# A graph-and-attention layer: seven of the eight q blocks made by seven products of halves, put together by VectorE

## The chip, the cores and the metric

The kernel runs on one core of a Trainium2 chip. The metric is the device time of one execution in microseconds (us); the kernel before has a median of 1512.12 us over three runs (1512.09 to 1512.35). Everything is float32. Engines are named as in the profile: PE is TensorE, DVE is VectorE, ACT is ScalarE, POOL is GpSimd, SP is the queue that issues most DMAs.

## What is computed

The input is x (4096 rows of 256) and a dense adjacency matrix of 4096 by 4096. Cut to what matters:

```python
h = layernorm(x) @ neigh_W.T
h = adj @ h / (adj.sum(axis=1, keepdims=True) + 1)
x = x + concat([layernorm(x), h]) @ lin_W.T        # the graph part

y = layernorm(x)                                   # one sequence of 4096
h = rmsnorm(y)
q, k, v = h @ wq.T, h @ wk.T, h @ wv.T             # 4 q heads, 2 k/v heads, 64 wide
q = q * cos + rotate_half(q) * sin                 # k likewise
att = causal softmax(q k / 8) v
y = y + att @ wo.T
out = x + y + mixture_of_8_experts(rmsnorm(y))     # the two best of a softmax router
```

rotate_half swaps the two halves of 32 of a head and negates the first.

## The kernel before

The 4096 rows are cut into eight blocks of 512. The first stage makes the graph part and, in its shadow, q, k and v; then follow attention and the experts. The change lies in the first stage alone, which on the timeline ends at about 510 us.

The stage is a loop over eight row blocks b. For each, `aggregate(b, steps)` (L516) adds up the products of eight adjacency blocks of 512x512, one for each step jb. A step does not make eight products of quarter blocks but seven (the scheme of Strassen and Winograd): `halve(n)` (L484) lets VectorE make the four sums S1, S2, S4 and S3 of a block's quarters (L495 to L498, each 128x512), S3 in place of A21; the g tiles hold the features and their sums. Each of the seven products is taken in two parts, k = 0 and 1 (L538), and in the profile each part is two instructions. The products fall into four PSUM banks. Steps 0 and 7 take the order `BY_BANK`, products 1, 2, 6, 7, 5, 3, 4, so that a bank after the other is done; they read A11, A12, S2, S3, S1, S4 and A22. At the end VectorE puts the seven together (L546 to L560).

The schedule is written out by hand: `tc.manual_schedule()` keeps every engine's instructions in the order of the code. In `aggregate` a step first calls `halve` for the block after it, so that VectorE makes the sums one step ahead; it then issues the seven products, and after the fourth it calls the functions that `steps` lists for this step. At the step's end come those listed under "end", the load of the adjacency block three further (three buffers, on SP), and those under "loaded".

What is listed for aggregate b is `qkv(b - 1)` (L573), which turns the row block just finished into q, k and v: step 1 the scales and tables, step 2 `norm` and `leave` (the normed rows go out to DRAM in `turning`), after step 2 `fetch` (they come back as 32x32 squares into `z`, which is room of a later qT, or `last_z` for b - 1 = 6), after step 3 `turn` (VectorE transposes z into qT[b], which now holds the normed rows with their features on the partitions), step 4 `values_and_logits` and `turned_heads((2,))` for k, step 5 `turned_heads((0, 1))` for the two halves of q. The eighth row block is made after the stage, in another way, by `rotated` and `heads`; the change does not touch it.

`turned_heads` (L644) makes 128 features of q or k by two products of 128x512 (L648) into a PSUM bank pj. VectorE multiplies pj by the cosines into its place, `to` (L655). ScalarE copies pj in four pieces of 32 partitions, swapped and with signs, into the tile `rot` (L657), of which there is one buffer (`bufs=1`). GpSimd multiplies rot by the sines (L661) and adds it to `to` (L662). Here `to` is qT[b] itself for q; its old content, the normed rows, has been read by then.

PSUM beside the four banks of the sums: two buffers tagged pj (`p_pj`) and two tagged tr (`p_tr`). They go round: `linear` (L195) takes one of each per half block at the end of step 0, `values_and_logits` two tr in step 4, k one pj in step 4, q two pj in step 5.

Weights: `load_rest` and `scale_rest` bring wq, wk and wv into wqkv_sb during aggregate 0; its last listed function is `router_wo` in step 7.

## Time and profile before

| | |
|---|---|
| median of three runs | 1512.12 us |
| the profiled execution | 1511.47 us |
| its span, first to last instruction | 1509.8 us |
| granted TensorE clock | 0.999 |
| TensorE busy | 1496.9 us, 99% |
| VectorE busy | 1083.9 us, 72% |
| ScalarE busy | 544.9 us, 36% |
| GpSimd busy | 568.9 us, 38% |
| q's products (L648, with k's) | 84 instructions, 592 ns each from issue to end |
| one product of the sums (L538) | 1792 instructions, 379 ns each from issue to end |

The profile is of one execution. Matmuls overlap in the pipeline: the distance from one start to the next is shorter than the 379 or 592 ns of one. A timeline row merges like instructions that follow each other: start, length of the whole row, engine, line, operation, tiles out<-in, shape and count; in brackets stands the idle time of the engine ahead of it and what ended it. The busy shares are means over stages of different kinds.

### The profile page before, as it was taken

How to read it: one execution, taken by the hardware profiler on the slowest of the kernel's cores; microseconds unless marked ns; L12 is line 12 of the kernel's file. 1: busy time of each engine (PE TensorE's matmuls, PEld its weight loads, DVE VectorE, ACT ScalarE, POOL GpSimd, SP SyncE). 2: the span in 40 equal slices, each digit the busy share in tenths (PEclk: the TensorE clock that was granted, in tenths of full speed). 3: DMA queues.
4: the chain of work that ended last, by engine and by line, in shares of the span. 5: the costliest groups of instructions: out<-in, count | busy, mean ns of one | idle time of the engine just before them, and what ended most of it. 6: DMA issues, size and time to landing. Idle time of an engine off the chain costs nothing. (4 is left out here: it accounts for less than half of the span.)

```text
span 1509.8 us, 28585 instructions
## 1 busy us (share of the span) xinstructions
PE 1496.9 (99%) x10731; PEld 1102.8 (73%) x10731; DVE 1083.9 (72%) x2239; ACT 544.9 (36%) x975; POOL 568.9 (38%) x649
## 2 busy tenths in 40 slices
PE   9999999999999999999999999999999999999997
PEld 7888888888888544444444444358899999999996
DVE  7855666656765577779879879795676877777872
ACT  2102011021020455655665655653222334343341
POOL 2102122121221331374565553551523464554542
PEclk9999999999999999999999999999999999999999
DMA  7435645555566000011010110029977898999965
GB/s 244 133 119 178 201 147 173 166 170 171 162 184 185 21 15 22 24 59 30 30 59 28 36 41 30 30 87 336 251 180 225 254 278 233 264 272 246 270 155 135
DMA packets 127005, 220.56 MB, mean 146 GB/s; under 512 B 79530, under 2 KB 103338, under 8 KB 113226
## 3 DMA queue, kind: packets, MB, share of 16 engines
q1 hardware_dynamic: 113322, 200.39, 42.3%
q0 software_dynamic: 12720, 17.47, 6.6%
q8 instruction: 86, 1.41, 0.4%
q10 hardware_dynamic: 816, 0.79, 0.2%
q14 instruction: 61, 0.50, 0.1%
HBM read 188.67 MB, written 31.33 MB: 146 GB/s over the span
## 5 line engine op out<-in xcount | busy, mean ns | idle before, releaser
L826 PE MATMUL sc<-qT_all,kT 64*64 64x512 f32 (+3 forms) x2304 | 282.1, 557 | 0.5 <-ACT pt_all L834 0.3
L538 PE MATMUL acc<-a,g 128*128 128x256 f32 x1024 | 244.0, 379 | 0.0
L538 PEld LDWEIGHTS acc<-a,g 128*128 128x128 f32 x1024 | 194.1, 190 | 32.2 <-issue 6.7
L826 PEld LDWEIGHTS sc<-qT_all,kT 64*64 64x64 f32 x2304 | 91.3, 133 | 128.9 <-issue 109.9
L834 ACT ACTIVATE pt_all<-sc 128x1024 f32<-128x1024 f32 (+3 forms) x157 | 149.0, 956 | 99.9 <-PE sc L826 95.6
L1917 POOL DMA_INDIRECT acc_dram<-y,late x40 | 63.3, 1583 | 177.0 <-ACT y L1906 118.9
L538 PE MATMUL acc<-more_sums,g 128*128 128x256 f32 x512 | 126.3, 379 | 0.0
L854 DVE TENSOR_TENSOR late<-late,pt_all 128x1024 f32<-128x1024 f32 (+3 forms) x92 | 106.6, 1159 | 20.4 <-ACT pt_all L834 9.0
L661 POOL TENSOR_TENSOR rot<-rot,tables 128x512 f32<-128x512 f32 x21 | 34.4, 1636 | 192.4 <-ACT rot L657 137.3
L538 PEld LDWEIGHTS acc<-more_sums,g 128*128 128x128 f32 x512 | 97.2, 190 | 13.2
L868 PE MATMUL y_second<-pt_all,vv 64*64 64x512 f32 (+3 forms) x440 | 105.0, 555 | 0.0
L868 PE MATMUL y_first<-pt_all,vv 64*64 64x512 f32 (+3 forms) x440 | 104.3, 553 | 0.0
L1837 PE MATMUL h<-late,qT_all 128*128 128x256 f32 (+1 forms) x616 | 104.0, 327 | 0.0
L1837 PEld LDWEIGHTS h<-late,qT_all 128*128 128x128 f32 x616 | 93.5, 191 | 9.6 <-ACT late L1521 0.8
L1110 POOL DMA_INDIRECT lists<-row,slots x64 | 91.3, 1426 | 17.2 <-issue 14.5
L636 ACT COPY vv<-pv 128x256 f32<-128x256 f32 x14 | 5.2, 373 | 251.9 <-PE pv L632 216.0
L868 PE MATMUL y_third<-pt_all,vv 64*64 64x512 f32 (+3 forms) x376 | 89.8, 557 | 0.0
L1844 DVE TENSOR_TENSOR late<-si,h 128x256 f32<-128x256 f32 (+2 forms) x87 | 39.3, 466 | 64.4 <-ACT si L1843 44.6
L657 ACT ACTIVATE rot<-pq 32x512 f32<-32x512 f32 x84 | 49.5, 589 | 82.5 <-DVE qT_all L655 33.1
L1843 ACT ACTIVATE si<-h 128x256 f32<-128x256 f32 (+2 forms) x87 | 36.1, 418 | 107.0 <-PE h L1837 93.1
L538 PE MATMUL acc<-qT_all,g 128*128 128x256 f32 x256 | 65.7, 379 | 0.0
L854 DVE TENSOR_TENSOR sum_all<-sum_all,pt_all 128x1024 f32<-128x1024 f32 (+3 forms) x49 | 53.5, 1093 | 15.8 <-POOL pt_all L836 9.9
(480 smaller groups left out, 3321.4 us busy)
## 6 DMA issues: line engine op xcount, KB each, us to landing
a<-in_adj_dram SPq DMA_DIRECT2D x64, 1024.0 KB
qT_all<-in_w_dram SPq DMA_DIRECT2D x18, 1408.0 KB
pt_all<-in_w_dram SPq DMA_DIRECT2D x16, 1408.0 KB
res_all<-in_w_dram SPq DMA_DIRECT2D x17, 768.0 KB
pt_all<-in_w_dram SPq DMA_DIRECT2D x16, 768.0 KB
res_all<-in_w_dram SPq DMA_DIRECT2D x8, 1408.0 KB
qT_all<-in_w_dram SPq DMA_DIRECT2D x9, 768.0 KB
late<-lists SPq DMA_DIRECT2D x96, 64.0 KB
```

The lines of the kernel that those rows point to most:

```text
L538: nc.tensor.matmul(acc[bank][:, at, :], g[jb][:, right, k, :], m[left][:, k, :], start=(jb == 0 and k == 0 and at == 0), stop=(jb == NB - ...
L657: nc.scalar.activation(rot[n * Q : (n + 1) * Q, :], pj[(n ^ 1) * Q : ((n ^ 1) + 1) * Q, :], AF.Copy, scale=1.0 if n % 2 else -1.0,)
L661: nc.gpsimd.tensor_mul(rot, rot, tables[b][:, 1, :])
L826: nc.tensor.matmul(ps[k * HP : (k + 1) * HP, j, :w], kT[sb][hd, i * P + k * HP : i * P + (k + 1) * HP], qT[b][hd, p, off:], start=True, st ...
L834: nc.scalar.activation(pt[:, :, :w], ps[:, :, :w], AF.Exp, scale=HD ** -0.5)
L854: nc.vector.tensor_add(sums[b, p][:, :, off:], before[:, :, off:], pt[:, :, : 512 - off])
L868: nc.tensor.matmul(accs[b, p][k][hd, off:], vv[sb][some, i, hd], pt[some, j, : 512 - off], start=(s == order_of(b)[0]), stop=(s == order_o ...
L1110: put = nc.gpsimd.indirect_dma_start(out=lists[:, :], out_offset=bass.IndirectOffsetOnAxis(ap=chosen[b][:, k, t, :], axis=0), in_=flats[b] ...
L1837: nc.tensor.matmul(ps[m % 2][:, m // 2 - q, :], w13_sb[:, c, m * P : (m + 1) * P], xT[:, c, :], start=(c == 0), stop=(c == 1),)
L1843: nc.scalar.activation(si[:, 0:both, :], ps[0][:, 0:both, :], AF.Silu)
L1844: nc.vector.tensor_mul(hT[:, q : q + both, :], si[:, 0:both, :], ps[1][:, 0:both, :])
L1917: put = nc.gpsimd.indirect_dma_start(out=(acc_dram if k < NM - LAST else out)[:, :], out_offset=at, in_=y[:, h, :], in_offset=None, comput ...
```

## The change

For row blocks 0 to 6 q is made by seven products of halves. The weights of q form a 2x2 of 128x128 pieces A11 to A22 (output half by input half), the normed rows a 2x2 of 128x256 pieces B11 to B22 (input half by columns). Once, in step 7 of aggregate 0, `sum_heads` has GpSimd make four sums of the weights. In step 4 of each following aggregate, ahead of the values, `sums_h` has VectorE make four sums of the rows in the room of z. In step 5 `seven_heads` takes the place of `turned_heads((0, 1))`: seven products of 128x256 into two pj and two tr banks; a copy by ScalarE and seven additions by VectorE, which write q over the rows in qT[b]; then the rotation of each half, which now reads q from SBUF: first ScalarE's four copies into rot, then VectorE's multiplication in place, then GpSimd's multiplication and addition. `last_z` becomes part of g[0], and the room freed holds the sums of the weights. k is made as before.

```diff
--- before.py
+++ after.py
@@ -386,6 +386,20 @@
             nc.scalar.copy(
                 wo_sb[:, :, C:], ps[:, 0 : 2 * NE].rearrange("p (j e) -> p j e", j=2)
             )
+
+        sums_q = gw.tile([P, 4, P], F32, name="sums_q")
+        heads_q = {
+            f"A{r + 1}{c + 1}": wqkv_sb[:, c, r * P : (r + 1) * P]
+            for r in range(2) for c in range(2)
+        }
+        heads_q.update((f"S{n + 1}", sums_q[:, n]) for n in range(4))
+
+        def sum_heads():
+            m = heads_q
+            nc.gpsimd.tensor_add(m["S1"], m["A21"], m["A22"])
+            nc.gpsimd.tensor_sub(m["S2"], m["S1"], m["A11"])
+            nc.gpsimd.tensor_sub(m["S3"], m["A11"], m["A21"])
+            nc.gpsimd.tensor_sub(m["S4"], m["A12"], m["S2"])
 
         def negate_weights():
             for k in range(2):
@@ -568,7 +582,7 @@
             )
 
         turning = [tc.dram_tile([512, C], F32, name=f"turning{n}") for n in range(2)]
-        last_z = gs.tile([P, 1024], F32, name="last_z")
+        last_z = g[0].rearrange("p n k i -> p (n k i)")[:, 0:1024]
 
         def qkv(b):
 
@@ -616,7 +630,7 @@
             def turn():
 
                 made["hT"] = qT[b]
-                z = made.pop("z").rearrange("p (m c d) -> p c m d", c=2, d=Q)
+                z = made["z"].rearrange("p (m c d) -> p c m d", c=2, d=Q)
                 for c in range(2):
                     nc.vector.transpose(
                         qT[b][:, c, :].rearrange("p (m i) -> p m i", i=Q), z[:, c]
@@ -640,6 +654,61 @@
                             first_lg[b][:, t, :], pj[:, i, 0:NE], AF.Copy,
                             scale=made["ratio"][:, t],
                         )
+
+            def sums_h():
+
+                m = made["m"] = {
+                    f"B{c + 1}{h + 1}": qT[b][:, c, h * 2 * P : (h + 1) * 2 * P]
+                    for c in range(2) for h in range(2)
+                }
+                room = made.pop("z").rearrange("p (n i) -> p n i", n=4)
+                m.update((f"T{n + 1}", room[:, n]) for n in range(4))
+                nc.vector.tensor_sub(m["T1"], m["B12"], m["B11"])
+                nc.vector.tensor_sub(m["T2"], m["B22"], m["T1"])
+                nc.vector.tensor_sub(m["T3"], m["B22"], m["B12"])
+                nc.vector.tensor_sub(m["T4"], m["T2"], m["B21"])
+
+            def seven_heads():
+
+                m = {**heads_q, **made.pop("m")}
+                banks = [
+                    p_pj.tile([P, 2, 2 * P], F32, tag="pj", name=f"pq_{b}_{n}") for n in range(2)
+                ] + [
+                    p_tr.tile([P, 2, 2, P], F32, tag="tr", name=f"pq_{b}_{n}").rearrange(
+                        "p c t i -> p c (t i)"
+                    ) for n in range(2, 4)
+                ]
+                p = {}
+                for n, (number, left, right) in enumerate((
+                    (1, "A11", "B11"), (2, "A12", "B21"), (6, "S2", "T2"), (7, "S3", "T3"),
+                    (5, "S1", "T1"), (3, "S4", "B22"), (4, "A22", "T4"),
+                )):
+                    p[number] = banks[n // 2][:, n % 2, :]
+                    nc.tensor.matmul(
+                        p[number], m[left], m[right], start=(n % 2 == 0), stop=True,
+                        skip_group_check=True,
+                    )
+                u2 = u4 = m["B12"]
+                u3 = m["B22"]
+                nc.scalar.copy(u2, p[1])
+                nc.vector.tensor_add(m["B11"], u2, p[2])
+                nc.vector.tensor_add(u2, u2, p[6])
+                nc.vector.tensor_add(u3, u2, p[7])
+                nc.vector.tensor_add(u4, u2, p[5])
+                nc.vector.tensor_add(m["B12"], u4, p[3])
+                nc.vector.tensor_sub(m["B21"], u3, p[4])
+                nc.vector.tensor_add(m["B22"], u3, p[5])
+                for k in range(2):
+                    to = qT[b][:, k, :]
+                    rot = gx.tile([P, 512], F32, tag="rot", name=f"rot_{b}_{k}", bufs=1)
+                    for n in range(4):
+                        nc.scalar.activation(
+                            rot[n * Q : (n + 1) * Q, :], to[(n ^ 1) * Q : ((n ^ 1) + 1) * Q, :],
+                            AF.Copy, scale=1.0 if n % 2 else -1.0,
+                        )
+                    nc.vector.tensor_mul(to, to, tables[b][:, 0, :])
+                    nc.gpsimd.tensor_mul(rot, rot, tables[b][:, 1, :])
+                    nc.gpsimd.tensor_add(to, to, rot)
 
             def turned_heads(ms):
                 pjs = [p_pj.tile([P, 512], F32, tag="pj", name=f"pq_{b}_{m}") for m in ms]
@@ -663,7 +732,7 @@
 
             return [
                 [scales, lambda: turn_tables(b)], [norm, leave], [],
-                [values_and_logits, lambda: turned_heads((2,))], [lambda: turned_heads((0, 1))],
+                [sums_h, values_and_logits, lambda: turned_heads((2,))], [seven_heads],
             ], {
                 (2, "end"): [fetch], (2, "loaded"): [lambda: spread_tables(b)],
                 (3, "end"): [turn],
@@ -705,7 +774,7 @@
                 steps[jb, "end"] = [lambda b=jb + 3: turned_x(b)]
         steps[0].insert(1, lambda: turned_x(2))
         steps[3].append(load_rest)
-        for jb, f in ((5, scale_rest), (6, bounds), (6, turn_wo), (7, router_wo)):
+        for jb, f in ((5, scale_rest), (6, bounds), (6, turn_wo), (7, router_wo), (7, sum_heads)):
             steps[jb].append(f)
         behind, at_end = [], []
         for b in range(NB):
```

## The prediction, made before the changed kernel was run

> **What bounds the kernel now.** I read the busy table and the groups first, to see who is never idle, then the timelines of four engines around one place where q is made. I chose the fifth of the seven (361 to 393 us): its adjacency block lands neither early nor late.

> ```profile
> PE 1496.9 (99%) x10731; PEld 1102.8 (73%) x10731; DVE 1083.9 (72%) x2239; ACT 544.9 (36%) x975; POOL 568.9 (38%) x649
> ...
> L661 POOL TENSOR_TENSOR rot<-rot,tables 128x512 f32<-128x512 f32 x21 | 34.4, 1636 | 192.4 <-ACT rot L657 137.3
> ...
> L657 ACT ACTIVATE rot<-pq 32x512 f32<-32x512 f32 x84 | 49.5, 589 | 82.5 <-DVE qT_all L655 33.1
> ```

> TensorE is the bound: 99% busy, so whatever its stream loses or gains is the kernel's time. In this stretch no TensorE row shows idle time at all, and q starts exactly 58.82 us after the one before (313.11, 371.93, 430.75). TensorE's timeline (start, us, row):

> ```profile
> 371.93 3.60 PE L648 MATMUL pq<-qT_all,wqkv_sb 128*128 128x512 f32 x8
> 375.36 1.03 PE L538 MATMUL acc<-a,g 128*128 128x256 f32 x4
> ...
> 383.13 2.75 PE L538 MATMUL acc<-a,g 128*128 128x256 f32 x12
> 385.72 1.03 PE L538 MATMUL acc<-more_sums,g 128*128 128x256 f32 x4
> 386.58 1.03 PE L538 MATMUL acc<-a,g 128*128 128x256 f32 x4
> 387.45 1.89 PE L538 MATMUL acc<-more_sums,g 128*128 128x256 f32 x8
> ```

> Each product of the program is two instructions. The row at 385.72 matters: it is the first in the last adjacency block (step 7) that reads a sum of VectorE's, S2; S3 is read at 386.58. VectorE's timeline:

> ```profile
> 374.70 0.69 DVE L655 TENSOR_TENSOR qT_all<-pq,tables 128x512 f32<-128x512 f32 x1 [3.59 <-PE pq L648]
> 375.56 0.69 DVE L655 TENSOR_TENSOR qT_all<-pq,tables 128x512 f32<-128x512 f32 x1 [0.17 <-PE pq L648]
> 376.17 0.68 DVE L495 TENSOR_TENSOR more_sums<-a 128x512 f32<-128x512 f32 x1
> 377.29 0.69 DVE L496 TENSOR_TENSOR more_sums<-more_sums,a 128x512 f32<-128x512 f32 x1 [0.44 <-PE acc L538]
> 378.02 0.69 DVE L497 TENSOR_TENSOR more_sums<-a,more_sums 128x512 f32<-128x512 f32 x1
> 378.62 1.76 DVE L498 TENSOR_TENSOR a<-a 128x512 f32<-128x512 f32 x1
> ```

> The sums for step 7 (L495 to L498) stand in VectorE's order directly behind the two rotation multiplies. S2 is ready at 377.98, 7.7 us ahead of its use. That 7.7 us is the cover to watch. ScalarE's and GpSimd's timelines:

> ```profile
> 375.51 2.39 ACT L657 ACTIVATE rot<-pq 32x512 f32<-32x512 f32 x4 [5.04 <-DVE qT_all L655]
> 381.54 2.39 ACT L657 ACTIVATE rot<-pq 32x512 f32<-32x512 f32 x4 [3.64 <-POOL qT_all L662]
> ```
> ```profile
> 378.05 1.79 POOL L661 TENSOR_TENSOR rot<-rot,tables 128x512 f32<-128x512 f32 x1 [4.47 <-DVE more_sums L496]
> 379.91 1.60 POOL L662 TENSOR_TENSOR qT_all<-qT_all,rot 128x512 f32<-128x512 f32 x1
> 384.07 1.54 POOL L661 TENSOR_TENSOR rot<-rot,tables 128x512 f32<-128x512 f32 x1 [2.56 <-ACT rot L657]
> ```

> rot has one buffer: ScalarE's second copy waits 3.64 us for GpSimd to finish with the first. Today only ScalarE and GpSimd carry that wait; VectorE's multiplies read PSUM and don't touch rot.

> [...]L498 takes 1.76 us beside L661 and 0.69 alone. [...]the rows above stand in the order of the code. [...]a ScalarE copy of 128x512 from PSUM took 586 ns (L439), one of 128x514 from SBUF 625 (L722).

> **The change, part by part.**

> TensorE's products. Out go 8 instructions of 128x512, 0.430 us apart ((3.60-0.592)/7), 3.44 us; in come 14 of 128x256, 0.216 apart ((2.75-0.379)/11), 3.02 us. Gain 0.42 us a block, 2.94 in seven. Weight loads rise from 8 to 14, 190 ns each, under the 216 between products as in L538's own rows.

> sum_heads: four GpSimd instructions of 128x128 once, in step 7 of aggregate 0. Between 0 and a 128x512's 1.27 us each; GpSimd sits idle for 20 us ahead of L661, so nothing waits[...]. Zero. last_z moved onto g[0]: fetch's DMAs are issued after step 2 and g[0] is last read in step 0; no queue waits. No DMA is added, and the tables' next load on SP comes at 390.74, after their last reader even in the case below.

> sums_h: four 128x256 adds ahead of kT's multiply (L655), some 1.7 us at 0.42 (rows L467 to L470). kT's multiply, ScalarE's rot and the release of its PSUM bank move back as much. That bank is the one that the third product of seven needs, 0.86 us after the start. Here: multiply to 369.7, ScalarE 369.8 to 372.2, needed at 372.79: no wait. In the first place (multiply 133.63 now, product 137.49) the wait is 1.1 us, in the third (250.84, 255.14) 0.6; the others have room. Together 1.7 us.

> The seven adds, and VectorE's new wait. The copy of p1 (0.37) and the first two adds hide behind the products. u3 overwrites B22, which the sixth product reads until 374.7. From there the critical chain:
> - u3, u4, B12: three adds 0.45 apart (as L547 to L549), to 376.1. ScalarE starts its first rot copy about there.
> - Four copies of 32x512, now from SBUF: 0.589 plus the 0.04 of the L722 comparison, 2.5 us, to 378.65. The in-place multiply of `to` must wait for them.
> - VectorE's multiply, GpSimd's multiply and add, then rot is free: 3.6 us (now 3.64), to 382.25.
> - Four copies of the second half, 2.5 us, to 384.75. VectorE's second multiply has been waiting at the head of its queue all this time; it ends at 385.5.
> - Only now S1 and S2 for step 7, queued behind it. GpSimd's multiply and add run just then, and the two engines take turns, as at 384.52 and 386.09 (1.64 and 1.75 us). S2 done 388.9, seen by TensorE at 389.0.

> TensorE, 0.42 ahead, wants S2 at 385.30: it stops for 3.7 us. S4 and S3 follow at 389.6 and 390.2, where S3 is wanted at 389.86: 0.45 more with the hand-over. So 4.15 us per block. Next late is L547, behind the next block's four sums (2.75 us), at about 393.4, and TensorE reaches its bank at about 393.6: just hidden. The last place has no following sums; the same otherwise.

> Sum: 7 × 4.15 + 1.7 - 2.94 = 27.8 us. The profiled execution took 1511.47 (span 1509.8 and 1.67 around it): 1539.3; it lies 0.65 under the median of 1512.12, so the forecast on that scale is 1540.

> **Bounds of what isn't shown.** Turn-taking: if GpSimd doesn't get between, S2 comes at 386.9 and the block loses 2.05 instead of 4.15: sum 13, or 1525. [...] ScalarE's SBUF copy: at its present 0.589, 0.3 us less a block; at double the extra, 0.3 more. Where ScalarE waits for all seven adds, not three, 0.8 more a block; where VectorE sees the sixth product one late, 0.4. Both: 1548. The clock: [...] I take none of it[...].

> **Rivals.**
> - Milder exclusion, 1525: for it, L496 at 383.80 ran in 0.69 beside a starting L661; against, both its successors paid.
> - Longer chain or half clock[...].
> - Hidden, faster: the rotation's chain stays off VectorE's queue, and 0.42 × 7 remains: 1509.2. The mechanism is the cover at step 7: S2 must be there at 385.3. It decides where the second multiply ends before 383.8 without turns, 1.7 us earlier than worked out, or before 381.8 with them. For it: today the same chain harms nobody, and VectorE is 72% busy. Against: ScalarE's 3.64 us wait for rot stays, and the multiply now can't precede ScalarE's reads.
> - A stall that just eats the gain, or a change that leaves the order as it was: 0.4 us a block, 1512.

> **How the numbers follow.** The measurement can tell about 0.2%, 3 us. Chances: forecast with turns 0.57, milder 0.18, longer 0.15, hidden 0.05, cancelling 0.05. Range: from the milder case to beyond both of the longer waits, 1524 to 1554, leaving out the hidden, the cancelling and part of the clock case. Faster 0.05, same 0.05, slower 0.90.

> **What would show it.** Right: L538's row that reads S2 in step 7 carries 2 to 5 us idle before it, released by VectorE's sums, seven times; the second in-place multiply shows a wait on ScalarE's rot of 5 us or so; q's products take 3.0 us instead of 3.44; q's distance grows from 58.82 to about 62.5. Wrong: TensorE without gaps in the stretch (the wait isn't where I put it), gaps at step 5 larger than 1 us (sums_h, or the banks, are the cost), the clock under 0.98 (half rate), or a step 7 whose sums were done before the rotation's multiplies (the order isn't the code's).

## The result, and the profile after

| | before | changed |
|---|---|---|
| median | 1512.23 us (4 runs, 1512.09 to 1513.57) | 1547.47 us (4 runs, 1543.34 to 1553.85) |
| profiled execution, its span | 1511.47, 1509.8 us | 1553.85, 1552.1 us |
| granted TensorE clock, profiled execution | 0.999 | 0.983 |
| distance from one q to the next | 58.82 us | 65.74, then 64.80 to 64.85 us |

The ratio is 1.0233, with a 95% interval of 1.0218 to 1.0248: slower by 35 us, 7.5 us more than the forecast of 1540 and inside the range of 1524 to 1554. Two things are new in the table: the runs spread over 10 us where those of before agree within 1.5, and the granted clock (the share of TensorE's full clock that it was given, as a mean over the span) fell. The changed execution's four clocks (0.983, 0.988, 0.990, 0.993) stand in the order of their times (1553.85, 1549.64, 1545.29, 1543.34).

The busy table and one group of the changed kernel's page (the last columns: idle time of the engine ahead of the group, and what ended it):

```profile
PE 1517.8 (98%) x10773; PEld 1125.9 (73%) x10773; DVE 1105.8 (71%) x2316; ACT 549.7 (35%) x982; POOL 563.0 (36%) x653
...
L552 PE MATMUL acc<-more_sums,g 128*128 128x256 f32 x512 | 142.5, 416 | 21.9 <-DVE more_sums L510 21.9
```

In the profile of before this group, L538 there, shows no idle time and a mean of 379 ns. Now TensorE stops for 21.9 us ahead of it, released by L510, which makes S2, and its instructions last 416 ns on average. TensorE's timeline around the second q shows both:

```profile
202.31 1.03 PE L687 MATMUL pq<-qT_all,wqkv_sb 128*128 128x256 f32 x4
203.18 1.89 PE L687 MATMUL pq<-qT_all,sums_q 128*128 128x256 f32 x8
204.91 0.59 PE L687 MATMUL pq<-qT_all,wqkv_sb 128*128 128x256 f32 x2
205.34 1.03 PE L552 MATMUL acc<-a,g 128*128 128x256 f32 x4
...
213.11 2.75 PE L552 MATMUL acc<-a,g 128*128 128x256 f32 x12
218.99 2.08 PE L552 MATMUL acc<-more_sums,g 128*128 128x256 f32 x4 [3.13 <-DVE more_sums L510]
220.85 1.91 PE L552 MATMUL acc<-a,g 128*128 128x256 f32 x4
222.56 3.13 PE L552 MATMUL acc<-more_sums,g 128*128 128x256 f32 x8
225.53 2.75 PE L552 MATMUL acc<-a,g 128*128 128x256 f32 x12
```

q takes 3.03 us (205.34 less 202.31) where it took 3.43 (375.36 less 371.93). At 218.99 stands the product that reads S2. The twelve instructions of the row before it are 0.216 us apart, so the next could have started at 213.11 + 12 × 0.216 = 215.70: the stop is 3.29 us. Then the four instructions last 2.08 instead of 1.03. From 218.99 to 225.53 sixteen instructions take 6.54 us; at 0.216 they take 3.45. The same stretch by windows of 2 us (sum; busy and instructions; granted clock; DMA share; GB/s):

```profile
215.00:217.00 2.00, 0.86 (x4) 1.00 0.97 283
217.00:219.00 2.00, 0.01 (x1) 0.81 0.58 242
219.00:221.00 2.00, 2.00 (x5) 0.50 0.00 0
...
225.00:227.00 2.00, 2.00 (x10) 0.98 0.00 0
```

The clock falls to half inside the stop and stays there until about 225; in windows of 0.02 us it is at half from 218.23 to 225.06, a spell of 6.83 us: 3.09 us lost a second time. Per place 3.29 + 3.09 - 0.42 = 5.96; from the second q to the third it is 64.80 less 58.82, 5.98. The stop is 3.29 or 3.30 us in all seven places of this execution, and the clock is halved in all seven. Only the first has a wait more, of 0.95 us within q's products.

VectorE, in the same place:

```profile
206.81 0.42 DVE L700 TENSOR_TENSOR qT_all<-qT_all,pq 128x256 f32<-128x256 f32 x1
209.13 0.69 DVE L709 TENSOR_TENSOR qT_all<-qT_all,tables 128x512 f32<-128x512 f32 x1 [1.90 <-ACT rot L705]
214.90 0.69 DVE L709 TENSOR_TENSOR qT_all<-qT_all,tables 128x512 f32<-128x512 f32 x1 [5.08 <-ACT rot L705]
215.51 1.75 DVE L509 TENSOR_TENSOR more_sums<-a 128x512 f32<-128x512 f32 x1
217.37 1.56 DVE L510 TENSOR_TENSOR more_sums<-more_sums,a 128x512 f32<-128x512 f32 x1
```

The two in-place multiplies (L709) wait for ScalarE 1.90 and 5.08 us; S1 and S2 (L509, L510) stand behind and, beside GpSimd, take 1.75 and 1.56 us where they take 0.69 alone: that is what the prediction's turns and exclusion come to here. ScalarE's row shows what the second multiply waits for:

```profile
206.56 2.54 ACT L705 ACTIVATE rot<-qT_all 32x512 f32<-32x512 f32 x4 [2.81 <-DVE qT_all L698]
212.33 2.54 ACT L705 ACTIVATE rot<-qT_all 32x512 f32<-32x512 f32 x4 [3.23 <-POOL qT_all L711]
```

### The profile page after: what moved, and what is told of

The parts are those of the page before. It is cut to its first block, busy times and chain, and to the rows that moved or that the text cites. A ratio compares the mean times of both kernels' runs of the same rounds, so it can differ in the third digit from the quotient of the medians.

```text
span 1552.1 us, 28809 instructions
## 1 busy us (share of the span) xinstructions
PE 1517.8 (98%) x10773; PEld 1125.9 (73%) x10773; DVE 1105.8 (71%) x2316; ACT 549.7 (35%) x982; POOL 563.0 (36%) x653
## 4 chain that ended last, share of the span: by engine, by line
PE 92%; ACT 3%; DVE 2%; POOL 2%; DMA 1%; issue 1%; SPq 0%; ACTq 0%; POOLq 0%; DVEq 0%
PE acc L552 22%; PE sc L895 15%; PE h L1906 13%; PE y_first L937 5%; PE y_second L937 5%; PE y_third L937 4%; PE ye_y L1960 4%; PE hA L1723 4%; PE ye_y L1863 3%; PE ye_ms L1863 2%; ACT rot L705 2%; PE hD L1723 2%; PE pf L523 2%; PE ph L199 2%; PE po L1017 1%; PE pq L687 1%
## 5 line engine op out<-in xcount | busy, mean ns | idle before, releaser
L552 PE MATMUL acc<-a,g 128*128 128x256 f32 x1024 | 250.2, 386 | 0.0
L552 PEld LDWEIGHTS acc<-a,g 128*128 128x128 f32 x1024 | 198.2, 194 | 31.0 <-issue 3.3
L552 PE MATMUL acc<-more_sums,g 128*128 128x256 f32 x512 | 142.5, 416 | 21.9 <-DVE more_sums L510 21.9
L552 PEld LDWEIGHTS acc<-more_sums,g 128*128 128x128 f32 x512 | 107.4, 212 | 41.9 <-DVE more_sums L510 24.7
L903 ACT ACTIVATE late<-sc 128x1024 f32<-128x1024 f32 (+3 forms) x55 | 50.7, 926 | 45.4 <-PE sc L895 41.9
```

Of the source, the lines that this page charges most:

```text
L552: nc.tensor.matmul(acc[bank][:, at, :], g[jb][:, right, k, :], m[left][:, k, :], start=(jb == 0 and k == 0 and at == 0), stop=(jb == NB - ...
L903: nc.scalar.activation(pt[:, :, :w], ps[:, :, :w], AF.Exp, scale=HD ** -0.5)
```

## The experiments

Theory Q is the prediction's: VectorE's queue is held by an in-place multiply that waits for ScalarE, which waits for the one rot buffer. Rival L: VectorE has too much work in these steps. Rival P: the sums and additions of the seven products make it late. The clock was taken as a cost of its own, to be told from the stop. Each median is compared with runs of the kernel before on the same chip: 1512.44 us for the first four kernels of the table, 1512.99 for the others.

| kernel | median, us | ratio, 95% interval |
|---|---|---|
| two rot buffers | 1517.77 | 1.0030 (1.0019 to 1.0042) |
| rotation a step later | 1519.47 | 1.0042 (1.0028 to 1.0057) |
| multiply aside | 1509.56 | 0.9978 (0.9970 to 0.9987) |
| gap filled by three products | 1537.12 | 1.0158 (1.0141 to 1.0175) |
| eight products, in place | 1534.83 | 1.0148 (1.0132 to 1.0163) |
| aside, sums of rows later | 1507.95 | 0.9966 (0.9954 to 0.9978) |
| eight products, aside | 1512.91 | 0.9995 (0.9986 to 1.0003) |
| gap shortened by one product | 1544.07 | 1.0208 (1.0193 to 1.0224) |

**Two rot buffers.**

```diff
-rot = gx.tile([P, 512], F32, tag="rot", name=f"rot_{b}_{k}", bufs=1)
+rot = gx.tile([P, 512], F32, tag="rot", name=f"rot_{b}_{k}", bufs=2)
```

The two other tiles with this tag get `bufs=2` as well.

> rot has two buffers, nothing else differs from the changed kernel. Theory Q (VectorE's queue: the second in-place multiply waits for ScalarE's second set of copies, these wait for the one rot buffer, and the sums for step 7 stand behind): the second set starts right behind the first, some 3.2 us earlier; GpSimd's four instructions then pile up beside S1 and S2, so S2 still comes about 0.9 us late instead of 3.29, S3 0.5 more, no half clock. 1512.2 - 2.9 + 1 + 7 x 1.4 = about 1520; at the best 1510. Rival L (VectorE has simply more work than step 5 to 7 hold, 4.6 us a block): the work is the same, so the 3.29 us gap and the half clock stay, about 1547.

1517.77. ScalarE's eight copies now run in one piece of 5.12 us, VectorE's second multiply starts 2.57 us after the first instead of 5.77, and S2 comes 0.55 us late, S3 0.46 more:

```profile
204.69 0.69 DVE L709 TENSOR_TENSOR qT_all<-qT_all,tables 128x512 f32<-128x512 f32 x1 [1.91 <-ACT rot L705]
207.26 1.15 DVE L709 TENSOR_TENSOR qT_all<-qT_all,tables 128x512 f32<-128x512 f32 x1 [1.88 <-ACT rot L705]
```

With no more than the length of the wait changed, 30 of the 35 us are gone: Rival L, with the same work, would have kept them.

**The rotation a step later.**

```diff
-                for k in range(2):
-                    to = qT[b][:, k, :]
+            def turn_heads():
+
+                for k in range(2):
+                    to = qT[b][:, k, :]
...
-                [sums_h, values_and_logits, lambda: turned_heads((2,))], [seven_heads],
+                [sums_h, values_and_logits, lambda: turned_heads((2,))], [seven_heads],
+                [turn_heads],
```

> The rotation of q is listed in step 6 instead of step 5, so that the sums for step 7 come ahead of its two multiplies in VectorE's order; all work is the same. Theory Q: the wait on ScalarE now has only the sums of the next block behind it, which are wanted a step later; no gap at step 7: 1512.2 - 2.9 + 1 (bank wait in the first place) = 1510, at most 3 us more if L561, behind the late sums, holds a bank at the block's start. Rival L: VectorE does the same work in the same steps, 1530 to 1547.

1519.47, ten above what theory Q expected; 3 us more was the most that was allowed for. VectorE's and TensorE's timelines say where it went:

```profile
210.88 0.69 DVE L711 TENSOR_TENSOR qT_all<-qT_all,tables 128x512 f32<-128x512 f32 x1 [4.11 <-ACT rot L707]
211.50 1.76 DVE L509 TENSOR_TENSOR qT_all<-a 128x512 f32<-128x512 f32 x1
213.36 1.57 DVE L510 TENSOR_TENSOR qT_all<-qT_all,a 128x512 f32<-128x512 f32 x1
...
216.17 0.41 DVE L561 TENSOR_TENSOR kT<-vv,acc 128x256 f32<-128x256 f32 x1
```
```profile
216.64 1.99 PE L552 MATMUL acc<-a,g 128*128 128x256 f32 x8 [1.34 <-DVE kT L561]
```

The stop at step 7 is gone, and the multiply still waits 4.11 us, now with the sums of the next block and L561 behind it. L561 reads the first PSUM bank, which the next block's first product wants: six stops of 1.3 to 1.4 us by the profile's count, 1.5 by the distance between starts, 9 us together. The margin that the prediction gave L561, 0.2 us, was too thin for a step's delay. So moving the held instructions only moved the stop; the queue is the cause, and what is queued behind decides who pays.

**Multiply aside.**

```diff
-                    nc.vector.tensor_mul(to, to, tables[b][:, 0, :])
+                    aside = made["aside"][:, k]
+                    nc.vector.tensor_mul(aside, to, tables[b][:, 0, :])
                     nc.gpsimd.tensor_mul(rot, rot, tables[b][:, 1, :])
-                    nc.gpsimd.tensor_add(to, to, rot)
+                    nc.gpsimd.tensor_add(to, aside, rot)
```

made["aside"] is the room of z, free again once the seven products have read the T sums.

> VectorE's multiply by the cosines writes into the room of the T sums instead of in place, and GpSimd adds from there; it no longer has to wait for ScalarE's reads. Same number, sizes and order of instructions. Theory Q: the two multiplies follow the seven additions at once, the sums for step 7 come some 6 us earlier, no gap: 1510. Rival L: the exclusion with GpSimd and the added work stay, so a gap of 1 to 3 us per block stays, 1520 to 1547.

1509.56: the whole loss is gone, and the median lies 2.9 us under that of before. Of this only 1.07 us are seen in the stage: by the traces attention starts at 506.71 instead of 507.78, since the bank that `sums_h` delays still costs something (two waits of 0.3 and 0.7 us and shorter ones). The work is the same, with one write moved. In VectorE's timeline the multiplies follow the additions at once:

```profile
200.60 1.28 DVE L711 TENSOR_TENSOR qT_all<-qT_all,tables 128x512 f32<-128x512 f32 x2
201.80 0.69 DVE L509 TENSOR_TENSOR more_sums<-a 128x512 f32<-128x512 f32 x1
202.59 0.69 DVE L510 TENSOR_TENSOR more_sums<-more_sums,a 128x512 f32<-128x512 f32 x1
```

Rival L expected a gap of 1 to 3 us; there is none.

**The gap filled.**

```diff
+                    if i == 1 and jb == NB - 1 and b:
+                        filler = p_tr.tile([P, 2, 2, P], F32, tag="tr", name=f"filler_{b}")
+                        for _ in range(3):
+                            nc.tensor.matmul(
+                                filler.rearrange("p c t i -> p (c t i)"), ident,
+                                wqkv_sb[:, 0, 0:512], start=True, stop=True,
+                            )
```

> Three products of 128x512 that nobody reads (2.6 us) are put into step 7 ahead of the product that reads S2, in the seven places; the rest is the changed kernel. They fill TensorE's gap, so its clock should not be halved, while S2 comes when it came. Theory Q with the clock as a second cost: per block 3.29 late plus 0.5 for S3 less 0.42, seven times and 1 for the first bank wait: 1512.2 + 24.5 = about 1536, with little spread between runs. Rival C (what follows the gap is slow for another reason, such as VectorE's lateness passed on): no gain, 1547 to 1550 and the product rows behind the gap still about twice as far apart.

1537.12, one above the figure expected, and four runs within 0.8 us. TensorE's timeline:

```profile
212.97 2.74 PE L561 MATMUL filler<-wqkv_sb,ident 128*128 128x512 f32 x6
216.26 1.13 PE L552 MATMUL acc<-more_sums,g 128*128 128x256 f32 x4 [0.55 <-DVE more_sums L510]
217.58 1.13 PE L552 MATMUL acc<-a,g 128*128 128x256 f32 x4 [0.20 <-DVE a L512]
```

S2 comes as late as in the changed kernel, but TensorE did work for nobody until 0.7 us before, and the products behind are 0.216 apart again; S3's own 0.46 us, which half rate had covered, comes to light (217.58 less 216.26 less 0.86). This throws out the rival named in the expectation, that what follows the stop is slow for another reason. Useless products made the kernel 10.35 us faster at the median: that is the net cost of the half clock, and the rest, 24.7 us over the kernel before, is the stops less what the products gain.

**The gap shortened.** The same edit with `range(1)`. It asks whether a shorter stop still halves TensorE's clock.

> One unread product of 128x512 (0.86 us) ahead of the product that reads S2, in place of three: TensorE's gap is about 2.4 us instead of 3.29, all else as in the changed kernel. [...] If part of the gaps of 2.4 us still halve it: between 1537 and 1555, 3.1 us less 0.5 for each gap that does, and the runs spread.

1544.07, 6.95 us above the filled gap. The gap is 2.43 us in all seven places (TensorE's timeline; two places of the seven):

```profile
217.77 1.13 PE L552 MATMUL acc<-more_sums,g 128*128 128x256 f32 x4 [2.27 <-DVE more_sums L510]
219.10 1.13 PE L552 MATMUL acc<-a,g 128*128 128x256 f32 x4 [0.20 <-DVE a L512]
280.39 1.13 PE L552 MATMUL acc<-more_sums,g 128*128 128x256 f32 x4 [2.27 <-DVE more_sums L510]
281.72 2.08 PE L552 MATMUL acc<-a,g 128*128 128x256 f32 x4 [0.20 <-DVE a L512]
```

In four places, as in the second of these, the clock is halved, shortly after the gap (four instructions in 2.08 us instead of 1.13); in three it isn't, and the two kinds alternate: the first, third, fifth and seventh place are hit. Such a spell is shorter here: windows of 20 us around the first, third and seventh have a granted clock of 0.91, which is about 3.6 us at half, and a place with a spell is 1.6 us longer than one without (63.91 and 62.28 us where no bank is waited for). So gaps 0.86 us shorter than those of the changed kernel do not escape the half clock.

The length alone does not decide: gaps of 2.43 us are hit in four places and not in three of the same execution, and gaps of 2.28 us, in the next version, in one of seven. What does decide was not shown.

**Eight products, in place.** `seven_heads` loses its products, copy and additions, and `sums_h` is not listed. In their place stand (the lines taken out are left out here):

```diff
+                for m, pj in enumerate(pjs):
+                    for c in range(2):
+                        nc.tensor.matmul(
+                            pj, wqkv_sb[:, c, m * P : (m + 1) * P], made["hT"][:, c, :],
+                            start=(c == 0), stop=(c == 1),
+                        )
+                for m, pj in enumerate(pjs):
+                    nc.vector.tensor_copy(qT[b][:, m, :], pj)
```

> The products of halves are undone: q is made by the four old products of 128x512, VectorE copies each bank into qT, and the rotation then runs from SBUF, in place, exactly as in the changed kernel; no sums of rows, no seven additions. Theory Q: the stall belongs to the in-place rotation in VectorE's queue, not to the products; ScalarE starts 0.75 us earlier and TensorE is 0.42 later than in the changed kernel, so S2 comes about 2.1 us late instead of 3.29, S3 0.5 more: 1512.4 + 7 x 2.6 = about 1531 without a half clock; 1550 if a gap of 2.1 us already halves it. Rival P (the seven additions and four sums are what makes VectorE late): no gap, 1512 to 1513.

1534.83, 3.8 us above the figure expected without half clock. The stop is there without any product of halves: 2.28 us before S2 (2.1 expected) and 0.46 before S3 in each of the seven places, and the half clock in one, this one (granted clock 0.91 from 210 to 230, 1.00 in the windows of 20 us around the other six):

```profile
210.23 0.69 DVE L690 TENSOR_TENSOR qT_all<-qT_all,tables 128x512 f32<-128x512 f32 x1 [5.08 <-ACT rot L686]
```
```profile
209.45 2.75 PE L552 MATMUL acc<-a,g 128*128 128x256 f32 x12
214.32 1.13 PE L552 MATMUL acc<-more_sums,g 128*128 128x256 f32 x4 [2.12 <-DVE more_sums L510]
215.65 1.65 PE L552 MATMUL acc<-a,g 128*128 128x256 f32 x4 [0.20 <-DVE a L512]
```

This throws out Rival P as the cause: the loss belongs to the second half of the change, the rotation in place from SBUF. The products of halves make the stop 1.0 us longer (3.29 less 2.28).

**Eight products, aside**, the same with the multiply into z's room:

> The eight products undone as in the in-place version, but VectorE multiplies aside, into the room of z. Theory Q: no gap; TensorE's stream is that of the kernel before: 1512.4. The difference to the kernel with seven products and sums later prices the products alone: 2.9 us. Rival P: the same 1512 as in the in-place version.

1512.91, the time of before within the interval, and q follows q at 58.82 us. The copies and the reads from SBUF cost TensorE nothing here once nobody is queued behind a wait.

**Aside, and the four sums of the rows behind k's multiply.**

```diff
-                [sums_h, values_and_logits, lambda: turned_heads((2,))], [seven_heads],
+                [values_and_logits, lambda: turned_heads((2,)), sums_h], [seven_heads],
```

> As the kernel that multiplies aside, and VectorE's four sums of the rows stand behind k's multiply instead of ahead of it, so that k's PSUM bank comes free 1.7 us earlier. Theory Q: TensorE's wait for that bank in the first places, about 1 us in all, goes: 1508.5, against 1509.6 with the sums ahead. If the bank wait was hidden, the same 1509.5.

1507.95: faster than both kernels. q follows q at 58.41 us in each place (before 58.82), where the version with the sums ahead varies between 58.41 and 59.26. By its trace attention starts 2.84 us earlier (504.94 against 507.78), and 2.77 earlier than with eight products aside (507.71), where 2.9 were expected for the products alone. The medians differ more, by 5.04 and 4.96 us; the other 2.2 lie outside the stage that the edit touches and are not explained here. The profiled executions of this kernel and of before are 3.43 us apart.

## Why the prediction was right, and the term that was too small

- **The products' gain**, 2.94 us: right. 3.43 to 3.03 us a place, and 7 × 0.41 = 2.87 in the distances of the last version.
- **The bank that sums_h delays**, 1.1 and 0.6 us: in part. In the first place product 6 starts at 138.38 instead of 137.43, 0.95 us late; in the third there was no wait. The version with the sums moved behind has no such wait at all.
- **The chain in VectorE's queue**: right in every link. Counted from q's first product, ScalarE's first copy was put at 4.2 us and came at 4.25; the copies at 2.5 and took 2.54; the wait for rot at 3.6 and took 3.23, since GpSimd's add had no VectorE instruction beside it (1.27 us); the second multiply's end at 13.6, measured 13.3; S2 at 17.0, measured 16.6. The stop came out at 3.29 where 3.7 was worked out. The turns with GpSimd were as priced (1.75 and 1.56).
- **S3's own wait**, 0.45: right at 0.46, but only to be seen where the clock isn't halved.
- **The sum without the clock**, 1540: the filled gap measured 1537.12. The distance of about 62.5 us was right for that kernel (62.3 where no bank is waited for), not for the changed one (64.80 to 64.85).
- **The clock**: the term that was mis-sized. The prediction took none of it; that was the author's estimate, and no run had shown it. In the profiled execution the stop of 3.29 us halved it in seven places of seven, for 6.83 us each, 3.09 lost. The measurement decides: gaps of 2.43 and 2.28 us did it in four and one of seven, gaps of 0.7 and 0.55 never (the four instructions that read S2, and the four behind them, last 1.13 us in all fourteen places; granted clock 0.999 and 0.998). The spell at 218.23 began 2.53 us after the stop did (218.23 less 215.70); in the seven places this distance is 2.41 to 2.66 us. At the median the clock adds 10.35 us, more than the 7.5 by which the forecast was passed, and the runs' times rise by 10.5 us as the granted clock falls from 0.993 to 0.983.
- **The signs**: "the clock under 0.98" was to show half rate. At 0.983 it wasn't met, with half rate in all seven places: 7 × 6.83 us at half is 1.5% of a span of 1552.1 us, so a mean over the span was too coarse a sign.
- **The rivals**: the milder exclusion is ruled out by the turns (1.75 and 1.56 us for S1 and S2, 0.69 alone). The half clock came true in part. The hidden rival would have needed the second multiply to end 1.7 us earlier than worked out, or 3.7 with the turns that GpSimd did take; it ended 0.3 earlier. It was made true by one changed operand, not by the change as it stood.

The total was helped a little by two misses of opposite sign: the stop was put 0.4 us too long, which makes 2.9 us in seven places, and the clock at nothing.

Why all seven places were hit is not explained. What the trace shows is steady: the seven spells begin at 153.38, 218.23, 283.09, 347.94, 412.79, 477.65 and 542.50, 64.85 us apart, and the distances from q to q stay within 64.80 to 64.85 us after the first. With gaps of 2.43 us every second place is hit, at distances that alternate (62.28 and 63.91 us where no bank is waited for). So "seven of seven" and "four of seven" need not be rates of a gap's length; no run varied the distance by itself. Left open: what decides whether a stop of 2.3 or 2.4 us is followed by half clock, and how many places were hit in the executions that were not profiled. By an estimate from the granted clock ((0.999 - 0.993) × 2 × 1541.6 us of half rate, at 6.83 us a place) it was about three in the fastest.

## What to carry to other kernels

An in-place operation on a tile that another engine still reads turned a hidden chain into a wait in the issuing engine's queue here (5.08 us at VectorE's second multiply); before making one, list what stands behind it and when that is wanted. If there is a room that is free by then, write aside: here that alone turned 35 us lost into 3 us won, by the medians. And price a stop on TensorE as more than its length: with 3.29 us of stop came some 3.1 of half clock, at each of the seven places of the profiled execution. A shorter stop was hit less often, but not never: 4 places of 7 at 2.43 us, 1 of 7 at 2.28.
